# All 64 quads written out, lane 1's sort placed behind lane 0's quads, and gathers of 128 successive edges

## The chip, the cores and the metric

The kernel runs on one core of one Trainium2 chip. The metric is the device time of one launch in microseconds. Most runs of one kernel agree within 0.3%; the three runs of the kernel before lie between 25,302.51 and 25,315.38 us, with a median of 25,311.82.

The engines are named as in the profile: PE is TensorE (PEld its weight loads), DVE is VectorE, ACT is ScalarE, POOL is GpSimd, SP is SyncE. Each takes its instructions in order, and they wait for each other through semaphores. SP and ACT issue plain DMAs; POOL issues the indirect ones, in which each of 128 partitions fetches its own row.

## The reference

A graph layer over V = 100,000 nodes with 64 channels and E = 3,300,000 edges (1.6 million random pairs in both directions, and a loop at each node), sorted by target:

```python
h = jnp.maximum(_layernorm(x, axis=-1), 0.0)
local, nbr = h[dst], h[src]
y = jnp.concatenate([local, nbr - local], axis=-1) @ W.T + b      # per edge
s = segment_sum(y, dst); cnt = segment_sum(ones, dst)
out = x + where(cnt > 0, s / maximum(cnt, 1), 0)
```

Since the layer is linear, it is enough to have, for each target, the sum of h[src] over its edges and the count; the two halves of W are applied once per node. On average a node has 33 edges, and their sources are random. So the work is a gather of 3.3 million rows and a sum over sorted targets.

## The kernel before

**Start.** h is computed and written to DRAM as `h3`, each value as three bf16 parts (192 columns, and a column of ones for the count: CE = 193). `bounds` reads the targets of all chunks (below) and finds each chunk's lowest target (`base_r`, `base_b`) and whether a chunk spans more than 128 nodes; if any assumption fails, a flag in `odd` sends the kernel through a general slow loop behind everything else (`n_slow`).

The edges are then summed in two ways.

**Windows, in quads.** The first 2,039,808 edges are cut into 256 windows of 7,968 successive edges (some 241 nodes each). Four windows make a quad, so there are 64 quads. The two *lanes* hold 128 windows each, one per partition. Three functions work on them:

- `sort_lane(l, ...)` (L432 on) loads a lane's targets and sources, packs both in one 32-bit key, and sorts the 8,192 keys of each partition by *source*, in a network of exchanges: ACT copies the lower half of a piece to `tmp` (L470), DVE writes the minimum and the maximum back (L471, L472). A piece has up to PIECE = 1536 elements, and `tmp` is in PSUM. Positions of block limits are counted by ACT (L548) and DVE (L603). The sorted keys go to DRAM (`ksort`).
- `fill_lane(l, ...)` (L636 on) fetches from `ksort`, for each of 157 blocks of 640 nodes, the keys of each window whose source is in the block (161 indirect DMAs at L651 and 64 at L736), and writes what the quads need to DRAM: source places `sr_d`, target places `dt_d`, and the rest `et_d`, `xs_d`.
- `quads(base, n, kept)` (L754 on) goes over 157 blocks and one last step per quad, two steps at a time ("a pair of steps"; 79 pairs a quad). SP loads a piece of the table of all rows (`tab`, 727.5 KB for three blocks; two loads more for `srs` and `dt`). DVE makes two one-hots, `gh` (L806) and `dh` (L348). TensorE picks rows by `gh` (L828, six matmuls of 128 x 128 per block), ACT casts the result to `gs` (L830), and TensorE adds it to the targets by `dh` (L836, sixteen matmuls of 32 rows per block). The last step adds the edges of a node to itself and the spilled keys, and takes the four sums out of PSUM, into tiles `wsums` (8 buffers) that SP writes to `acc`. With `kept`, one table piece in five stays in SBUF.

**Chunks, by gathers.** The other 1,260,192 edges are cut into 352 chunks of 3,584 edges. `chunks(first, n, dynamic)` (L353 on) gives each partition 28 successive edges. Gather j (L403, an indirect DMA on POOL) takes edge j of each partition: 128 rows of `h3`. A one-hot `hot` of 128 x 128 for each gather (L348; DVE makes 14 at a time, a half chunk, in 4 buffers) gives the target relative to the chunk's lowest, and a matmul adds the rows to 128 sums (L408). `nb`, the gathered rows of a half chunk, has 6 buffers, so POOL runs up to six halves ahead of TensorE. There are 352 x 28 = 9,856 gathers.

**Order.** `sort_lane`, `fill_lane`, `quads` and `chunks` are generators: each `yield` hands back to the code that interleaves them, and a planner then puts the instructions in an order on each engine, close to that of the program, but with those ahead that are ready early; `issue_after(last[...])` (`behind()`) pins some to their places. The order is:

1. Lane 0's sort with gathers (`gathers(ns)`: one gather per GATHER = 1250 ns of the yields' own estimates), then lane 1's sort with lane 0's fill and gathers. Each lane has its own `keys` buffer.
2. Quads 0 to 3 with lane 1's fill and gathers; then the rest of the first PA = 70 chunks.
3. A loop `For_i` of three rounds: each holds 20 quads written out, and 94 chunks spread over them. Quad and chunk numbers are registers there.

The last lines of step 3 in the code:

```python
with tc.For_i(0, (SETS - U0) // SB, 1) as g:
    last.clear()
    ev = chunks(None, KB, PA + g * KB)
    next(ev)
    owed = 0.0
    for _ in quads(U0 + g * SB, SB, kept):
        owed += 2 * (KB * J - 1) / (SB * NE)
        while owed > 0:
            next(ev, None)
            owed -= 1
    drain(ev)
    add_now(True)
```

**End.** Rows shared by neighbouring windows or chunks are added, the means are taken and multiplied by the second half of W, and the result is written (L1065 to L1085).

## Time and profile before

| | us |
|---|---|
| median of three runs | 25,311.82 |
| lowest and highest run | 25,302.51, 25,315.38 |
| the profiled execution: its run | 25,318.98 |
| the profiled execution: span, first to last instruction | 25,317.3 |

The profile is of one execution. Busy time is the union of an engine's instructions; a matmul's end is modelled. "Idle before" is an engine's time without work just before a group, with what ended it: "<-issue" means that no semaphore was waited for, "<-remote" that the profile doesn't know who. The granted TensorE clock has a mean of 0.723. Three groups that the change touches, from the page's list of the costliest (line, engine, operation, output<-input, shapes, count | busy us, mean ns | idle us before, who ended it):

```profile
L403 POOL DMA_INDIRECT nb<-h,si x9856 | 9337.3, 947 | 13259.9 <-PE ps L408 8539.2
...
L348 DVE TENSOR_TENSOR hot<-near,c 128x1792 bf16<-128x1792 int16 x704 | 759.5, 1079 | 113.6 <-remote 107.4
...
L651 POOL DMA_INDIRECT kf<-ksort,at_i x322 | 306.6, 952 | 205.8 <-ACT k L692 108.3
```

### The profile page before, as it was taken

How to read it: one execution, taken by the hardware profiler on the slowest of the kernel's cores; microseconds unless marked ns; L12 is line 12 of the kernel's file. 1: busy time of each engine (PE TensorE's matmuls, PEld its weight loads, DVE VectorE, ACT ScalarE, POOL GpSimd, SP SyncE). 2: the span in 40 equal slices, each digit the busy share in tenths (PEclk: the TensorE clock that was granted, in tenths of full speed). 3: DMA queues.
4: the chain of work that ended last, by engine and by line, in shares of the span. 5: the costliest groups of instructions: out<-in, count | busy, mean ns of one | idle time of the engine just before them, and what ended most of it. 6: DMA issues, size and time to landing. Idle time of an engine off the chain costs nothing. (4 is left out here: it accounts for less than half of the span.)

```text
span 25317.3 us, 562905 instructions
## 1 busy us (share of the span) xinstructions
PE 14841.3 (59%) x238778; PEld 10732.9 (42%) x238778; DVE 11321.0 (45%) x15478; ACT 6060.7 (24%) x11710; POOL 10302.7 (41%) x10609
## 2 busy tenths in 40 slices
PE   4100365466666666665666666666566666666666
PEld 3000244344444444444444444444444444444445
DVE  6878443243444444443444444444344444444444
ACT  4333221122222222221222222222222222222222
POOL 5666533433333333334333333333333333333334
PEclk6555577677777777777777777777777777777777
DMA  6722354354454454454444544444445444444446
GB/s 227 102 46 46 100 172 147 108 151 143 145 149 145 147 149 143 149 153 134 147 143 147 149 146 148 149 147 145 138 144 148 145 150 146 150 145 145 148 145 231
DMA packets 1671411, 3615.08 MB, mean 143 GB/s; under 512 B 951932, under 2 KB 960263, under 8 KB 1663911
## 3 DMA queue, kind: packets, MB, share of 16 engines
q1 hardware_dynamic: 1225338, 3006.63, 36.6%
q0 software_dynamic: 335040, 507.40, 10.5%
q10 hardware_dynamic: 108492, 64.90, 1.3%
q8 instruction: 1874, 30.70, 0.5%
q14 instruction: 667, 5.46, 0.1%
HBM read 3397.56 MB, written 219.36 MB: 143 GB/s over the span
## 5 line engine op out<-in xcount | busy, mean ns | idle before, releaser
L403 POOL DMA_INDIRECT nb<-h,si x9856 | 9337.3, 947 | 13259.9 <-PE ps L408 8539.2
L348 DVE TENSOR_TENSOR dh<-dt,c 128x1024 bf16<-128x1024 int16 x5056 | 3450.9, 683 | 12561.4 <-remote 7908.4
L830 ACT CAST gs<-gp 128x386 bf16<-128x386 f32 x10048 | 4786.8, 482 | 16980.7 <-remote 9615.5
L836 PE MATMUL total<-gs,dh 32*128 32x193 bf16 x160768 | 6254.9, 264 | 4279.4 <-issue 4266.3
L828 PE MATMUL gp<-tab,gh 128*128 128x193 bf16 x48408 | 6076.5, 270 | 2426.6 <-issue 2187.6
L828 PEld LDWEIGHTS <-gh 128*128 128x128 bf16 x60288 | 5384.1, 105 | 4772.8 <-issue 4394.3
L836 PEld LDWEIGHTS <-dh 32*128 32x128 bf16 x160768 | 3875.8, 99 | 6281.3 <-issue 6228.6
L806 DVE TENSOR_TENSOR gh<-srs,c 128x1536 bf16<-128x1536 int16 x5056 | 4760.5, 942 | 15.0 <-issue 7.9
L408 PE MATMUL ps<-nb,hot 128*128 128x193 bf16 x9856 | 1934.7, 281 | 2839.1 <-DVE sums L422 1230.1
L408 PEld LDWEIGHTS <-hot 128*128 128x128 bf16 x9856 | 1048.8, 111 | 3031.1 <-DVE sums L422 1261.7
L828 PE MATMUL gp<-kept,gh 128*128 128x193 bf16 x11880 | 1551.9, 274 | 505.0 <-issue 493.1
L470 ACT COPY tmp<-keys 128x1536 f32<-128x1536 f32 (+14 forms) x540 | 649.6, 1212 | 1324.0 <-DVE keys L472 602.4
L348 DVE TENSOR_TENSOR hot<-near,c 128x1792 bf16<-128x1792 int16 x704 | 759.5, 1079 | 113.6 <-remote 107.4
L471 DVE TENSOR_TENSOR keys<-tmp,keys 128x1536 f32<-128x1536 f32 (+14 forms) x540 | 756.6, 1420 | 88.8 <-ACT junk L548 41.4
L472 DVE TENSOR_TENSOR keys<-tmp,keys 128x1536 f32<-128x1536 f32 (+14 forms) x540 | 756.3, 1419 | 22.4 <-issue 7.1
L795 POOL DMA_INDIRECT rows_x<-h,xs x128 | 120.8, 944 | 985.0 <-DMA xs<-xs_d 930.5
L651 POOL DMA_INDIRECT kf<-ksort,at_i x322 | 306.6, 952 | 205.8 <-ACT k L692 108.3
L856 DVE SCALAR_TENSOR_TENSOR whole<-own,whole 128x193 f32<-128x193 bf16 x512 | 190.3, 413 | 88.3 <-ACT whole L852 87.8
L420 DVE TENSOR_REDUCE sums<-ps 128x64 f32<-128x192 f32 x349 | 122.1, 350 | 209.5 <-remote 197.0
L310 PE MATMUL o_ps<-w_own,hT 128*128 128x128 f32 x784 | 186.7, 376 | 14.4 <-ACT hT L305 13.8
L310 PEld LDWEIGHTS o_ps<-w_own,hT 128*128 128x128 f32 x784 | 154.8, 251 | 77.8 <-ACT hT L305 68.2
L736 POOL DMA_INDIRECT kx<-ksort,xat x128 | 120.7, 943 | 88.5 <-DVE xat L733 43.5
(184 smaller groups left out, 3297.5 us busy)
## 6 DMA issues: line engine op xcount, KB each, us to landing
tab<-tables SPq DMA_DIRECT2D x2668, 727.5 KB
srs<-sr_d SPq DMA_DIRECT2D x1216, 512.0 KB
nb<-h,si POOLq DMA_INDIRECT x9856
tables<-h ACTq DMA_DIRECT2D x157, 242.5 KB
h<-parts SPq DMA_DIRECT2D x28, 1358.0 KB
acc<-zeros SPq DMA_DIRECT2D x28, 910.0 KB
at<-acc SPq DMA_DIRECT2D x28, 910.0 KB
xt<-in_x SPq DMA_DIRECT2D x28, 896.0 KB
```

The lines of the kernel that those rows point to most:

```text
L310: nc.tensor.matmul(o2[:, i], lhsT=hT[:, i], rhs=w_own.rearrange("p a c -> p (a c)"), start=False, stop=True)
L348: nc.vector.tensor_tensor(out.rearrange("p k (a d) -> p k a d", d=D), numbers[:, :, None].to_broadcast(shape), upto[:shape[0], :n].rearran ...
L403: last[POOL] = nc.gpsimd.indirect_dma_start(out=nb[:, j], out_offset=None, in_=h3, in_offset=bass.IndirectOffsetOnAxis(ap=si[:, u, at:at + ...
L408: nc.tensor.matmul(ps, lhsT=before[0][:, j], rhs=before[1][:, j, :CE], start=before[2] == 0 and j == 0, stop=before[2] == parts - 1 and j ...
L470: last[ACT] = nc.scalar.copy(tmp, lo)
L471: nc.vector.tensor_tensor(lo, tmp, hi, ALU.min)
L472: last[DVE] = nc.vector.tensor_tensor(hi, tmp, hi, ALU.max)
L651: last[POOL] = nc.gpsimd.indirect_dma_start(out=kf[:, c], out_offset=None, in_=ksort, in_offset=bass.IndirectOffsetOnAxis(ap=at_i[:, c0 + ...
L806: nc.vector.tensor_tensor(gh[:, :m].rearrange("p c i b s -> p (c i) b s"), srs[u, s // SL][:, c:c + m].rearrange("p c i s -> p (c i) s")[: ...
L828: nc.tensor.matmul(gp[:, i], lhsT=ghots[t][:, i, b], rhs=row[:, b + i * (NB - NR), :CE], start=b == 0, stop=b == NR - 1)
L830: nc.scalar.copy(gs[t], gp)
L836: nc.tensor.matmul(total[:, i, to(b)], lhsT=hot[at, b * P:b * P + P], rhs=of[at], start=flags.get("start", False) and b == 0, stop=flags.g ...
```

## The change

- **Gathers.** A gather takes 128 successive edges of a chunk in place of one edge from each of 128 runs (the host lays `src_p` and `dst_p` out anew). Its targets then lie near 4j above the chunk's lowest, so the one-hot is only BAND = 32 columns wide, relative to that drift. It is written into a strip of zeros (four tiles `narrow`, kept for the whole kernel), and the matmul reads a window of 128 columns of the strip, placed so that the band falls on the right targets. `bounds` checks the band in place of the span. The buffers of `nb` go from 6 to 5.
- **Order.** Only lane 0 is sorted ahead of the quads. Quads 0 to 31 follow, written out: lane 0's fill runs beside quad 0, ahead of it by two pieces, and lane 1's sort and fill run behind the rest (`behind_quads`), paced by their estimates. In lane 1's sort (`soft`) the pieces are of 1,024, `tmp` is a single buffer in SBUF, the copy on ACT and the minimum and maximum on DVE are two pairs of steps apart, no order is pinned, and ACT makes all the counts. There is one `keys` buffer for both lanes.
- Then quads 32 to 63, written out, with the kept tables, and the remaining gathers spread evenly. There is no loop, so no number of a quad or a chunk is a register.
- `dh` gets 5 buffers and also holds the one-hots of the last step, four at a time (`eh` had its own tile); `wsums` goes from 8 buffers to 5; quad 0 loads what its last step needs later (`late`).

```diff
-SB = 20
-KB = 94
-U0 = 4
+PARTS = (32, 32)
+U1 = 32
-STEP = 1300
+STEP = 2200
+BEHIND = 1.0
+BAND = 32
-EXTRA = 350
-PIECE = 1536
+PIECE = (1536, 1024)
-PART = 1024
+PART = 512
...
+            e = pre.tile([P, CHUNK], I32, name="e", bufs=1)
+            nc.vector.tensor_tensor(e[:n].rearrange("c (p j) -> c p j", j=J), d[:n].rearrange("c (p j) -> c p j", j=J),
+                                    drift_i[:n, None, :].to_broadcast([n, P, J]), ALU.subtract)
+            nc.vector.tensor_reduce(off[:n, 1, m:m + 1], e[:n], axis=AX.X, op=ALU.min)
...
+                nc.vector.tensor_sub(rel[:, :k], rel[:, :k], drift[:, None, :].to_broadcast([P, k, J]))
...
+            narrow = [[few.tile([P, JH * (P + D) + JH * D], BF16, name=f"hot{part}{i}") for i in range(2)]
+                      for part in range(J // JH)]
+            for hot in narrow[0] + narrow[1]:
+                nc.vector.memset(hot, 0.0)
...
-                    hot = rows.tile([P, JH, P], BF16, name="hot", bufs=4)
+                    hot = narrow[part][q % 2]
                     nb = rows.tile([P, JH, CT], BF16, name="nb")
                     with behind():
-                        one_hot(hot, near[:, u, part * JH:part * JH + JH], P)
+                        one_hot(hot[:, part * JH * D:][:, :JH * (P + D)].rearrange("p (k x) -> p k x", x=P + D)[:, :, :BAND],
+                                near[:, u, part * JH:part * JH + JH], BAND)
...
-                        nc.tensor.matmul(ps, lhsT=before[0][:, j], rhs=before[1][:, j, :CE],
+                        nc.tensor.matmul(ps, lhsT=before[0][:, BAND // 2 + j * P:BAND // 2 + j * P + P], rhs=before[1][:, j, :CE],
...
             def exchange(lo, hi, tmp):
-                last[ACT] = nc.scalar.copy(tmp, lo)
-                nc.vector.tensor_tensor(lo, tmp, hi, ALU.min)
-                last[DVE] = nc.vector.tensor_tensor(hi, tmp, hi, ALU.max)
+                ins = nc.scalar.copy(tmp, lo)
+                if not soft:
+                    last[ACT] = ins
+
+                def finish():
+                    nc.vector.tensor_tensor(lo, tmp, hi, ALU.min)
+                    ends_at(nc.vector.tensor_tensor(hi, tmp, hi, ALU.max))
+
+                return finish
+
+            def both(part, n):
+                finish = part()
+                if soft:
+                    yield 0
+                    yield 0
+                finish()
+                yield 2.083 * n + 290
...
+                    dh = hots.tile([P, 2, 2, CH], BF16, name="dh", bufs=5)
...
+                    begin = fill_lane(0, fill, took)
+                    for _ in range(4 * SL):
+                        next(begin)
+                    rest = behind_quads()
+                    left = 0.0
+                    for i, _ in enumerate(quads(0, U1, late=True)):
+                        if i < NE // 2 - 10:
+                            for _ in range(4):
+                                next(begin, None)
+                            gathers(STEP / 2)
+                        else:
+                            drain(begin)
+                            left += BEHIND
+                            while left > 0:
+                                left -= 1 + next(rest, 0) / 1500
+                            gathers(STEP)
                     drain(rest)
...
+                pace = (NCH * J - count[0]) / ((SETS - U1) * NE // 2 - 4)
+                owed = 0.0
+                for _ in quads(U1, SETS - U1, kept):
+                    gathers(pace * GATHER)
+                drain(ev)
+                add_now(True)
...
+    def by_gather(a):
+        return np.ascontiguousarray(a.reshape(nch, J, P).transpose(0, 2, 1))
```

`took()` counts each fetch of keys as a gather, so gathers pause while a lane is filled.

## The prediction

> **What bounds the kernel now.** I read the page's busy times first, then a table of windows by stage, then the timeline inside the loop, because no engine on the page is full.
>
> ```profile
> PE 14841.3 (59%) x238778; PEld 10732.9 (42%) x238778; DVE 11321.0 (45%) x15478; ACT 6060.7 (24%) x11710; POOL 10302.7 (41%) x10609
> ...
> q8 instruction: 1874, 30.70, 0.5%
> ```
>
> Busy shares give no bound here. The table by stage (start and end, length, then busy time and count of PE, PEld, DVE, ACT, POOL, granted clock, DMA share, GB/s) shows where the time is: lane 0's sort, lane 1's sort, the four quads ahead of the loop, leftover gathers, the loop, the tail.
>
> ```profile
> 430.00:1601.00 1171.00, 119.74 (x739) 103.71 (x740) 1047.49 (x989) 427.33 (x466) 768.36 (x787) 0.53 0.51 84
> 1601.00:2768.00 1167.00, 95.96 (x554) 73.45 (x552) 862.35 (x1146) 397.43 (x448) 757.79 (x798) 0.52 0.25 46
> 2768.00:4290.00 1522.00, 901.77 (x14225) 629.88 (x14223) 654.56 (x1127) 344.37 (x673) 609.86 (x644) 0.71 0.56 164
> 4290.00:4640.00 350.00, 70.66 (x655) 53.89 (x656) 41.23 (x72) 7.90 (x17) 219.44 (x234) 0.56 0.23 49
> 4640.00:24942.00 20302.00, 13185.85 (x219861) 9464.68 (x219861) 8305.74 (x11673) 4578.33 (x9654) 7531.60 (x7981) 0.75 0.49 146
> 24942.00:25318.00 376.00, 199.29 (x1184) 180.02 (x1181) 145.31 (x261) 57.06 (x115) 211.34 (x64) 0.76 0.73 277
> ```
>
> Sixty of the 64 quads fill 20,302 us, 338 us each. Two neighbouring windows in the loop, and POOL's timeline there, say why:
>
> ```profile
> 15074.00:15090.00 16.00, 15.69 (x314) 13.09 (x315) 11.93 (x17) 6.64 (x14) 0.94 (x1) 0.86 0.67 195
> 15090.00:15108.00 18.00, 6.68 (x53) 2.74 (x50) 1.71 (x3) 0.96 (x2) 12.26 (x13) 0.65 0.47 135
> ```
>
> ```profile
> 15088.79 0.94 POOL L403 DMA_INDIRECT nb<-h,si  x1 [17.14 <-PE ps L408]
> 15090.04 0.94 POOL L403 DMA_INDIRECT nb<-h,si  x1 [0.31 <-issue]
> ```
>
> With POOL quiet, TensorE starts 314 matmuls in 16 us; while POOL issues gathers, 53 in 18 us, and it waits for no semaphore ("issue"). The gathers come in bursts of 14, one every 1.25 us, when TensorE has freed a half chunk's rows (the wait for PE ps). I counted matmul starts from the records between 4800 and 11,200 us: inside bursts (shifted by 2.5 us, since data moves after the issue) 2.2 per us, outside 19.05. So gathers and quads nearly exclude each other, and the time is a sum of two prices. A quad has 3,666 matmuls (2,592 of L836, 942 of L828, 132 of L408): 3,666/19.05 = **192.4 us a quad**. A gather takes 1.25 x (1 - 2.2/19.05) = **1.10 us of TensorE** if it falls beside quads, and none beside a sort. Check: 60 x 192.4 + 7,981 x 1.10 = 20,323 against 20,302, loop starts included. The four early quads: 770 + 644 x 1.10 = 1,478 against 1,522. The loop alone would fit 1.08, so I use 1.09.
>
> **The change, part by part,** against the profiled span of 25,317.3 us (its run took 25,318.98, the median of three is 25,311.8, so 6 us come off at the end).
>
> *Lane 1's sort leaves the front.* Quads start at 2768 now. They can start when lane 0's sort is done and the first piece is filled. Lane 0's first fetch from the sorted keys is issued at 1601.6, but 146 us of lane 1's DVE work was done before it (29 of its exchanges at 2 x 1.43 us, 46 us of its load, 17 us of its reductions). With one keys buffer that work comes later; DVE is 89% busy in the stage, so I take 110 of the 146. Eight fetches, their DVE work and two DMAs: some 35 us more. Start at about 1,525: **-1,243**. Bounds: -1,100 (nothing of the 146) to -1,290.
>
> *More gathers fall beside quads.* The number of gathers stays 9,856. The sort's yields add up to 870,100 ns, one gather per 1,250 ns: 696 are issued behind lane 0, and I take 710 with those that run ahead. So 9,146 fall beside quads, with both lanes' 450 fetches of keys (225 a lane, 322 + 128 in all) and the 128 of rows_x: 9,724 against 644 + 7,981 = 8,625. 1,099 x 1.09 = **+1,198**. Bounds: the price from 1.07 to 1.25, +1,176 to +1,374. Their forms (128 rows of 194 bf16 from random sources) don't change: successive edges share a target, not a source.
>
> *The leftover gathers (4290 to 4640) go*: 350 us in which TensorE had almost no quad work; the 234 gathers are in the count above. The new seam after quad 31, where pools are opened again, I set at 50 by the loop starts: **-300** (-350 to -250).
>
> *The loop goes.* The windows with its second and third start hold 5,161 and 5,030 matmuls, their neighbours 5,450 and 5,440; at 10.9 per us that is 27 and 38 us: **-65** (-65 to 0). Written-out code costs no fetches: 1,874 packets of 16 KB carry 64 B for each of TensorE's 477,556 instructions, so the loop's code was fetched anew every time round already.
>
> *The one-hot of 32 columns.* Now 128 x 1792 elements in 1,079 ns, 704 times. A quarter of it is 448 elements, and the dh of 512 elements takes 421 ns, so about 0.4 us: 0.68 us saved a time, 480 us of DVE. But DVE waits for TensorE at nearly every dh (0.4 to 0.5 us), so most is hidden; in 5,000 us of the loop TensorE waits about 130 us for DVE in all. I take **-60** (-250 to 0). The weights stay 128 columns wide, so TensorE's price is unchanged. The extra subtraction in load is 44 x 0.4 us, hidden by DVE's slack.
>
> *Lane 1's sort and fill run behind quads 0 to 31.* 327,679 element pairs in 339 pieces of up to 1,024: 678 min/max at about 1.15 us (1,024 elements take 1.215) = 780 us; load 60; the fill's DVE rows add up to 210: **1,050 us on DVE**, and 339 copies of about 1 us plus 146 us of counts on ACT. The pacing spends 2,016 of 2,459 pairs of steps on it. DVE needs 1.46 us a pair (gh and dh start 0.86 and 0.60 apart), TensorE 192.4/79 = 2.44, so 0.94 x 2,459 = 2,300 us of slack covers it. What is not covered: DVE runs in order, so a 2.3 us min/max delays the next gh, behind which TensorE's L828 waits; its lead is one to two pairs, and more with dh's five buffers. ACT's copy likewise stands ahead of a gs cast. Bounds 0 (all in the lead) to +1,050 (all exposed); the nearest row is 2768 to 3200, where a fill with 210 us of DVE ran beside 2,500 matmuls (131 us at 19.05) and 227 indirect DMAs (247 us). That makes 378 of 432 us; of the 54 left a part is the quads' start, so at most a quarter of the fill showed. I take a fifth: **+200**.
>
> *Lane 1's tmp is in SBUF, lane 0's in PSUM.* Beside a DVE operation with two SBUF inputs a gather is longer:
>
> ```profile
> 485.88 0.94 POOL L403 DMA_INDIRECT nb<-h,si  x1 [0.30 <-issue]
> 486.64 1.23 DVE L458 TENSOR_TENSOR own<-s,keys 128x1024 int32<-128x1024 int32 x1 [4.93 <-DMA s<-in_src_w]
> 487.13 1.56 POOL L403 DMA_INDIRECT nb<-h,si  x1 [0.31 <-issue]
> ```
>
> 0.62 us more. Bursts fill half of the first 32 quads, but DVE mostly waits in them: 678 x 0.25 x 0.62 = **+105** (0 to +420).
>
> The Trainium skill ("SBUF — State Buffer", Who interferes with whom) speaks against this move: a DVE instruction with two SBUF inputs contends with a GpSimd one that reads SBUF, and the later is blocked for the whole of the other. The 1.56 agrees in kind, not in size; by its full 1.15 us a time the term would be +195 instead.
>
> *Quad 0* fetches its keys while it runs, and its last step needs xs and et, which come behind 31 us of DVE (64 x 0.48) and 64 fetches of 1.25 us: **+60** (0 to +150). *The bounds* read each chunk once more, 3 passes of DVE beside loads: **+10** (0 to 30).
>
> Sum: -1,243 + 1,198 - 300 - 65 - 60 + 200 + 105 + 60 + 10 = -95: 25,222 in the profile's terms, **25,215** as a median, 0.4% faster.
>
> **The rivals.** *The sort is not hidden* (slower). Place: DVE's queue in quads 1 to 26. For it: DVE's 1.46 plus the sort's 0.43 to 0.52 a pair is close to the 2.07 us in which a pair runs when TensorE is warm. Against it: the row of 2768 to 3200. Half exposed: 25,215 + 525 - 200 = 25,540; all, 26,065. It turns the sign from 297 us exposed.
> *The sort is free*: it fits into bursts in which DVE sits still and lengthens none: 25,215 - 305 = 24,910. For it: in 5,000 us of the loop DVE stands at dh for 1,816 us, 151 times. Against it: it waits at dh, with the sort's pieces queued behind.
> *Tables*: quads 4 to 31 lose the kept fifth, 28 x 11 x 727.5 KB = 224 MB, 560 us at the 400 GB/s of busy slices; half unhidden gives 25,495. Against it: from 3400 to 4280, without kept tables, 19.1 matmuls per us outside bursts as in the loop.
> *Not what it says*: the gathers stop disturbing TensorE because of their new order. Half the price would be 19,900; nothing in the trace speaks for it, as the sources stay random.
>
> **How the numbers follow.** My sum 0.50 (its own range 25,080 to 25,360), not hidden 0.27, free 0.16, tables 0.05, the gathers' price gone 0.02. 24,900 to 25,650 takes the first whole, most of the free case and the tables, and the cheaper part of the exposed one. About 0.2% (50 us) can be told from no change: faster below 25,261: 0.64 of the first, the free one, the last: 0.50; within: 0.13; slower: the rest, 0.37.
>
> **What would show it.** Lane 0's first fetch of keys near 1,490, the first L828 near 1,525. Outside bursts 19 matmuls per us in the second half; in the first half 18 if the sort costs 200, 15 or less if it is exposed, with PE's L828 waiting for DVE gh or keys. Gathers beside keys' min/max over 1.5 us. I am wrong if a gather's 1.10 us differs, or if POOL issues far more than 710 gathers ahead of the quads.

## The result

| | us |
|---|---|
| before: median of 4 runs (range) | 25,307.17 (25,299.20 to 25,315.38) |
| after: median of 4 runs (range) | 171,500.22 (171,485.17 to 171,528.44) |
| ratio, 95% interval | 6.7769 (6.7651 to 6.7886) |
| after: the profiled execution's span | 171,493.9 |

The forecast was 25,215 us. The changed kernel takes nearly seven times as long. Its page says at once where. The rows of the slices that matter, and the first two of its groups (count | busy us, mean ns | idle before, who ended it):

```profile
span 171493.9 us, 888195 instructions
...
PE   4666650000000000000000000000000000000000
...
POOL 4334444444444444444444444444444444444444
...
L1098 POOL DMA_INDIRECT acc<-sums,ti x25792 | 40201.6, 1559 | 56741.3 <-ACT sums L1097 44966.4
L1076 POOL DMA_INDIRECT nb<-h,si x25792 | 31111.8, 1206 | 17865.3 <-DMA si<-in_src_a 10495.2
```

TensorE has work in the first six slices of forty and next to none in the others. The two groups have 25,792 instructions each and are not on the page of before at all. 25,792 = 1,612 x 16: they are the 16 gathers and the 16 accumulating stores of each round of the general loop (L1066 to L1098), the second way of computing the sums, which runs only when a flag in `odd` says that the fast way can't be trusted. Windows by stage of the changed kernel (start:end, length, then busy time and count of PE, PEld, DVE, ACT, POOL, granted clock, DMA share, GB/s): lane 0's sort, the quads with lane 1's sort, two stretches of the other quads, the end of the quads, then two windows behind them:

```profile
430.00:1600.00 1170.00, 125.53 (x759) 106.53 (x757) 900.55 (x967) 395.09 (x446) 771.98 (x817) 0.53 0.47 88
1617.00:4900.00 3283.00, 1856.33 (x27926) 1313.24 (x27927) 2050.79 (x3040) 1084.02 (x1973) 1172.65 (x1191) 0.73 0.50 147
4900.00:13300.00 8400.00, 5485.61 (x90858) 3895.53 (x90855) 3308.10 (x4901) 1892.35 (x3992) 3094.08 (x3280) 0.75 0.55 170
13300.00:24850.00 11550.00, 7295.22 (x112388) 5048.52 (x112388) 4084.65 (x6144) 2315.12 (x4894) 4742.85 (x5028) 0.72 0.45 135
24850.00:25206.00 356.00, 238.82 (x4146) 173.91 (x4147) 145.16 (x227) 83.49 (x176) 118.85 (x126) 0.76 0.49 141
25206.00:171110.00 145904.00, 8105.16 (x25805) 2656.72 (x25796) 22331.20 (x37088) 4105.39 (x25784) 71296.66 (x51574) 0.50 0.17 27
171110.00:171494.00 384.00, 202.73 (x1184) 182.33 (x1183) 140.01 (x236) 58.08 (x124) 227.82 (x75) 0.75 0.72 271
```

The sixth window is 145,904 us long: 1,612 rounds of 90.5 us. What is left is 25,206 + 384 = 25,590 us, 273 more than the 25,317.3 of before. So there are two things to explain: a flag that should not be set, and a remainder 1.1% slower where 0.4% faster was foretold. In the timeline of one round the accumulating stores stand one behind the other, some 3.9 us apart; each waits for sums that DVE makes only when the store four places ahead has landed (four buffers):

```profile
100000.78 1.56 POOL L1098 DMA_INDIRECT acc<-sums,ti  x1 [2.40 <-ACT sums L1097]
100004.01 0.36 DVE L1096 TENSOR_REDUCE sums<-ps 128x64 f32<-128x192 f32 x1 [3.52 <-DMA acc<-sums,ti]
100004.40 0.16 ACT L1097 COPY sums<-ps 128x1 f32<-128x1 f32 x1 [3.72 <-DVE sums L1096]
100004.69 1.55 POOL L1098 DMA_INDIRECT acc<-sums,ti  x1 [2.36 <-ACT sums L1097]
```

**Which flag.** The change gives `bounds` a new question: does each gather of 128 edges stay in its band of 32 columns? For the low side it takes, over all places of a chunk, the smallest (target - 4 x number of the gather), and sets the flag where `least` - that - 1 reaches 16. I worked this out from the edges themselves. In 351 of the 352 chunks the value is at most 7 on the low side and 6 on the high side, less than half of the limit. The last chunk has 2,208 edges; its other 1,376 places are filled with target V = 100,000. Its least target is 99,932. The filled places of gather 27 give 100,000 - 4 x 27 = 99,892, and 99,932 - 99,892 - 1 = 39: the flag is set. The change masks the filled places for the high side (`d < V` times e, ahead of the max), but the min stands before the mask.

Each group of the runs below had the kernel before beside it on the same chip, and in two groups of five the kernel before took about 15,400 us, in the other three about 25,600, like the 25,307 above; ratios are formed within a group.

### The profile page after: what moved, and what is told of

Same layout as the page of the kernel before. It is cut to its first block, busy times and chain, and to the rows that moved or that the text cites. A ratio compares the mean times of both kernels' runs of the same rounds, so it can differ in the third digit from the quotient of the medians.

```text
span 171493.9 us, 888195 instructions
## 1 busy us (share of the span) xinstructions
PE 23572.7 (14%) x264570; PEld 13599.5 (8%) x264570; DVE 33268.4 (19%) x52824; ACT 10177.3 (6%) x37719; POOL 81637.6 (48%) x62195
## 3 DMA queue, kind: packets, MB, share of 16 engines
q0 software_dynamic: 4874432, 2649.99, 13.5%
q8 instruction: 1872, 30.67, 0.1%
## 5 line engine op out<-in xcount | busy, mean ns | idle before, releaser
L1098 POOL DMA_INDIRECT acc<-sums,ti x25792 | 40201.6, 1559 | 56741.3 <-ACT sums L1097 44966.4
L1076 POOL DMA_INDIRECT nb<-h,si x25792 | 31111.8, 1206 | 17865.3 <-DMA si<-in_src_a 10495.2
L1094 PE MATMUL ps<-nb,same 128*128 128x193 bf16 x25792 | 8106.7, 332 | 137830.8 <-DVE same L1080 66492.3
L1096 DVE TENSOR_REDUCE sums<-ps 128x64 f32<-128x192 f32 x25792 | 9161.2, 356 | 87234.3 <-DMA acc<-sums,ti 87234.2
L418 POOL DMA_INDIRECT nb<-h,si x9856 | 9348.3, 948 | 13436.6 <-PE ps L423 10453.5
L1094 PEld LDWEIGHTS <-same 128*128 128x128 bf16 x25792 | 2657.0, 109 | 143276.6 <-DVE same L1080 73066.9
L1097 ACT COPY sums<-ps 128x1 f32<-128x1 f32 x25792 | 4105.7, 159 | 141845.5 <-DVE sums L1096 141543.0
L869 PE MATMUL gp<-tab,gh 128*128 128x193 bf16 x53952 | 7092.2, 275 | 3596.1 <-issue 2867.3
L869 PEld LDWEIGHTS <-gh 128*128 128x128 bf16 x60288 | 5509.1, 106 | 6176.3 <-issue 5581.3
L1080 DVE TENSOR_TENSOR same<-dr,di 128x2048 bf16<-128x2048 int32 x1612 | 5742.3, 3562 | 0.0
L1083 DVE TENSOR_TENSOR prior<-same,before 128x2048 f32<-128x2048 bf16 x1612 | 3694.7, 2292 | 55.5
L1085 DVE TENSOR_REDUCE first<-prior 128x16 f32<-128x2048 f32 x1612 | 3669.3, 2276 | 0.0
L869 PE MATMUL gp<-kept,gh 128*128 128x193 bf16 x6336 | 878.2, 279 | 411.2 <-issue 361.2
```

What stands on the lines that cost most here:

```text
L418: last[POOL] = nc.gpsimd.indirect_dma_start(out=nb[:, j], out_offset=None, in_=h3, in_offset=bass.IndirectOffsetOnAxis(ap=si[:, u, at:at + ...
L869: nc.tensor.matmul(gp[:, i], lhsT=ghots[t][:, i, b], rhs=row[:, b + i * (NB - NR), :CE], start=b == 0, stop=b == NR - 1)
L1076: nc.gpsimd.indirect_dma_start(out=nb[:, j], out_offset=None, in_=h3, in_offset=bass.IndirectOffsetOnAxis(ap=si[:, j:j + 1], axis=0))
L1080: nc.vector.tensor_tensor(same, dr.rearrange("q p j -> q j p"), di[:, :, None].to_broadcast([P, JA, P]), ALU.is_equal)
L1083: nc.vector.tensor_mul(prior, same, before[:, None, :].to_broadcast([P, JA, P]))
L1094: nc.tensor.matmul(ps, lhsT=same[:, j], rhs=nb[:, j, :CE], start=True, stop=True)
```

## Experiments on the flag

**pads** (15,400 group): the changed kernel with one constant changed.

```
-        "dst_p": by_gather(padded(dst[n:], nch * CHUNK, V)),
+        "dst_p": by_gather(padded(dst[n:], nch * CHUNK, V + P)),
```

> The changed kernel, with the 1,376 empty places behind the last chunk's 2,208 edges filled with target V + P instead of V. Theory 1 (the padding trips the new band check): with V, the last chunk's least target is 99,932 and its smallest target less 4 x gather number is 100,000 - 108 = 99,892, so least - that - 1 = 39, over the limit of 16; with V + P it is at most 7, no flag is set, the general loop does no round, and the time is that of the changed kernel's quads plus its tail: 25,206 + 375 = 25,580 (25,400 to 25,750). Rival 2 (another flag, or a chunk whose edges really leave the band): the general loop still runs its 1,612 rounds, 171,500.

Measured: 16,433.99 us, ratio 1.0681 (1.0664 to 1.0698). The page of pads has no group of the general loop: the padding sets the flag, and nothing else does. The absolute number was foretold for a chip on which the kernel before takes 25,310, and is no test of it. **pads_2** repeated it in a 25,600 group.

> The padded version once more. Where the kernel before takes 15,400: 16,434 again. Where it takes 25,600: the twin with a third buffer for si and xs took 1.0142 of it, and the part of the changed kernel's own profile ahead of the general loop, 25,206 + 375, gives 1.011; theory: 1.010 to 1.016. Rival (the third buffers saved time there too): above 1.02.

Measured: 25,922.24 us beside 25,566.96, ratio 1.0143 (1.0125 to 1.0161), inside its range. This is the change with its flaw mended: 1.4% slower.

**forced** (15,400 group): the kernel before, with its flag set always.

```
-            nc.vector.tensor_scalar(odd[:, 0:1], odd[:, 0:1], float(P), None, op0=ALU.is_ge)
+            nc.vector.tensor_scalar(odd[:, 0:1], odd[:, 0:1], 1.0, None, op0=ALU.is_ge)
```

> The kernel before, with the limit of its span check lowered from 128 to 1 so that the flag is always set and the general loop computes the sums once more. Theory 1: the price of the general loop has nothing to do with the new order or gathers: 25,310 + 1,612 x 90.45 = 171,100 within 1%. Rival: the changed kernel's state makes the loop slow; then clearly less here.

Measured: 162,114.47 us, which is 146,714 over the 15,400.1 of before, 91.0 us a round beside 90.5. The general loop costs the same in the old order. My number for the sum was 5% too high, because it was made with the other base.

## Experiments on the remainder

**order_only** and **gathers_only** (15,400 group) take the change apart. order_only is the changed kernel with the old gathers, one-hots and check; gathers_only is the kernel before with the new ones, and V + P as fill.

```
 order_only
-                    hot = narrow[part][q % 2]
+                    hot = rows.tile([P, JH, P], BF16, name="hot", bufs=4)
...
-        "src_p": by_gather(padded(src[n:], nch * CHUNK, 0)),
+        "src_p": padded(src[n:], nch * CHUNK, 0).reshape(nch, P, J),
 gathers_only: the same places, the other way round, in the kernel before
```

> The changed kernel with the old gathers: edges spread over a chunk by column as before, one-hots of 128 columns, the old check of the span. No fill of the last chunk can trip that check. Theory 1: 25,630 (the padded version's 25,580 plus the 50 that the prediction gave to the narrow one-hot and its check). Rival 2 (the new order of the work, not the band check, sets a flag): 171,500. Rival 3 (the narrow one-hot costs time): below the padded version.

> The kernel before, in its old order with its loop, with the new gathers alone (128 successive edges, 32 columns, the band check, empty places at V + P). The prediction's terms give 25,310 - 60 + 10 = 25,260 (25,060 to 25,340): DVE saves 0.68 us 704 times, mostly hidden. Rival: DVE's queue paces the loop more than was thought, then up to -480: 24,830. If the gathers disturbed TensorE less in their new order, far less than 24,800.

Measured: order_only 16,477.73, ratio 1.0705 (1.0686 to 1.0724), so 44 us above pads; gathers_only 15,379.73 beside 15,400.1, ratio 0.9987 (0.9975 to 1.0000). Both put the narrow one-hot and its check at a gain of 20 to 44 us, beside the -60 + 10 of the prediction. In that group all of the loss, 1,034 us in pads, is the order's. Neither was run in a 25,600 group, so there it is not shown.

**half_old**, **half_new**, **half_old_2** leave out every second gather of the loop (half_old, 3,948 of them) or of the changed order behind the 28th chunk (half_new, 4,536), with the matmuls kept. These three were run once each, and so were forced, rows64 and nokept_old.

```
-                        last[POOL] = nc.gpsimd.indirect_dma_start(
+                        if dynamic is None or j % 2 == 0:
+                            last[POOL] = nc.gpsimd.indirect_dma_start(
...
-                        nc.tensor.matmul(ps, lhsT=before[0][:, j], rhs=before[1][:, j, :CE],
+                        nc.tensor.matmul(ps, lhsT=before[0][:, j], rhs=before[1][:, j if dynamic is None else j - j % 2, :CE],
```

> The kernel before; in its loop each second gather is left out, and the matmul of an edge row that was not fetched reads its neighbour's row instead (so the sums are others; the number of matmuls is the same). Some 3,950 gathers fewer. On a chip where the kernel before takes 15,400, theory: gathers take nothing from TensorE there (20 matmuls per us while they run), so 15,300 to 15,450. On one where it takes 25,310, theory: 1.09 each, 21,000; rival, 1.27 to 1.40 each as the quads of the changed kernel fit: 20,300 to 19,800. Rival for the first: GpSimd's 1.25 us each holds the loop there too, then some 5 per cent less.

> The padded version; from the 29th chunk on each second gather is left out and the matmul of an edge row that was not fetched reads its neighbour's row (other sums, same number of matmuls): 4,536 gathers fewer. Theory (GpSimd's issue holds quads 33 to 62): they fall from 215 to the 183 to 187 us of the old loop, quads 7 to 31 from 207 to about 198 as in the old order without kept tables, 1,100 us in all: 15,200 to 15,400. Rival (gathers are as free as they were in the old order, 147 us for 3,950; the order of DVE's work or the tables set the quads): 16,250 to 16,350.

> The kernel before with each second gather of its loop left out (3 x 94 x 14 = 3,948; the matmul of an edge row that was not fetched reads its neighbour's row). Where the kernel before takes 25,600: at the prediction's 1.09 us a gather 4,300 less, 21,300; at the 1.3 that leaving out 4,536 gathers of the new order showed, 5,130 less, 20,470. Where it takes 15,400: 15,262 again.

Measured: half_old (15,400 group) 15,261.90 beside 15,408.84: 147 us for 3,948 gathers, 0.04 us each. There a gather costs the quads nothing. half_old_2 (25,600 group) 20,422.97 beside 25,566.96: 5,144 us, **1.30 us a gather**, not 1.09. half_new fell in a 25,600 group, for which its text had no number: 20,060.23, which is 5,904 below si3 of the same group, again 1.30 each. So the prediction's price was a fifth too low for the gathers at the margin, and its ranges for the price (1.07 to 1.25) did not reach it.

**rows64** (25,600 group): each gather behind the 28th chunk fetches 64 rows, not 128.

```
+                        m = P if q < 28 else P // 2
                         last[POOL] = nc.gpsimd.indirect_dma_start(
-                            out=nb[:, j], out_offset=None, in_=h3,
-                            in_offset=bass.IndirectOffsetOnAxis(ap=si[:, u, at:at + 1], axis=0))
+                            out=nb[:m, j], out_offset=None, in_=h3,
+                            in_offset=bass.IndirectOffsetOnAxis(ap=si[:m, u, at:at + 1], axis=0))
```

> The padded version; from the 29th chunk on each gather fetches 64 rows and not 128, and its matmul uses those 64 alone, so that half of these edges are left out of the sums; the number of gathers and of matmuls is the same. Where the kernel before takes 25,600: if the price of a gather goes by its rows (their descriptors or packets), 9,072 x 0.65 = 5,900 less than the padded version; if it goes by the instruction, within 300 us of it. Where it takes 15,400: 0 to 300 less than the padded version by either, as fewer packets share the DMA engines with the tables.

Measured: 26,431.24, which is 509 above pads_2 and not 5,900 below it. So halving the rows and the bytes does not lower the price. The packets are not halved: on the gathers' queue their number is the same in both runs, and only the time that they took is less (first pads_2, then rows64; packets, packet time in us, share):

```profile
q0 software_dynamic: 335040, 507.40, 10.2%
q0 software_dynamic: 335040, 282.12, 6.5%
```

Whether the price goes by the instruction or by its packets is therefore not told apart. That the time rose by 509 agrees with neither number; in the trace quads 7 to 62 are each some 9 us longer, and I have no cause for it.

**lanes3** (25,600 group) follows from that price: the kernel before with 96 quads and 1,904 gathers instead of 64 and 9,856.

```
-LANES = 2
-SB = 20
-KB = 94
+LANES = 3
+SB = 23
+KB = 2
...
-                add_later((LAG - 1) * J, put)
-                add_later((LAG - 1) * J + GAP, shared)
+                put()
+                shared()
```

> The kernel before with three lanes of windows and not two: 96 quads, 68 chunks and not 352 (1,904 gathers, 1,680 of them ahead of the loop), 4 rounds of 23 quads with 2 chunks each, and a quad's rows stored as soon as they are summed. Where the kernel before takes 25,600, theory (a gather beside quads 1.30 us, a quad alone 169): quads start 1,168 later, at 3,936; 96 x (169 + 7.5 for 5 to 6 DMAs) = 16,950; 390 for the last lane's fill beside the first quads, 132 for four starts of the loop, 376 behind: 21,780 (21,300 to 22,300). Rival (1.09 and 192.4, the prediction's split): 96 x 198.5 = 19,060, so 23,890. Where it takes 15,400 and a quad takes 183 us with its gathers for nothing: 22,600.

Measured: 22,112.59 us, ratio **0.8652** (0.8637 to 0.8666): faster than the kernel before and than even_3 (25,828) in that group, and inside its range of 21,300 to 22,300. Ten of its quads, with 20 indirect DMAs in all (window; columns as above):

```profile
6460.00:8250.00 1790.00, 1545.35 (x35286) 1274.86 (x35289) 1275.88 (x1751) 767.94 (x1608) 18.86 (x20) 0.93 0.73 238
```

A quad nearly alone takes 179 us, at 35,286 / 1,790 = 19.7 matmuls per us. With the 132 matmuls of its share of gathers (6.7 us at that rate) it would be 186. That corrects both splits: the prediction's 192.4 was 6 too high, and the 169 of lanes3's text is no quad alone but the foot of a line through quads with many gathers. The price per gather grows: from 186 to the 257 us that quads of half_old_2 take with 68 indirect DMAs it is 1.05 us each, and from there 1.30 for each one that the kernel before has more. The 1.05 is an estimate, a mean over the first 68 from traces of different groups: within half_old_2 the quads that are neither first nor last in a round have 58 to 79 indirect DMAs and lie on 1.14 to 1.31 us each, depending on where a quad is cut, so the low price belongs to the first ones. Why it grows is open. Where the kernel before takes 15,400, lanes3 was not run; at its text's 22,600 it would be far slower there.

**pinned** and **pace** (15,400 group) and **si3** and **even** (25,600 groups) ask what the order itself costs.

```
 pinned: the min and max of lane 1, and its copies likewise behind the gs cast
+        def at_quads(soft, of):
+            return tc.issue_after(last[of].ins) if soft and of in last else nullcontext()
...
+                    with at_quads(soft, "dh"):
                         nc.vector.tensor_tensor(lo, tmp, hi, ALU.min)
                         ends_at(nc.vector.tensor_tensor(hi, tmp, hi, ALU.max))
 pace
-STEP = 2200
+STEP = 2400
 si3 (and xs likewise)
-                si = index.tile([P, KG, J], I32, name="si")
+                si = index.tile([P, KG, J], I32, name="si", bufs=3)
 even: si3, STEP 2350, yield 1500 behind each fetch of keys, and
+                            if i == NE // 2 - 10:
+                                owed = 0.0
...
-                                left -= 1 + next(rest, 0) / 1500
+                                with tc.issue_after(last["dh"].ins):
+                                    left -= 1 + next(rest, 0) / 1500
```

> The padded version (fill V + P) with each piece of lane 1's sort tied behind the quad's own work at which it is written: its copy behind that pair's gs cast on ACT, its min and max behind that pair's dh on DVE. The order then has the 339 pieces in quads 1 to 21 and not all in quads 1 to 5. Theory (DVE is full in quads 1 to 6 because the sort was drawn together there): quads 1 to 6 fall from some 310 us and more to some 220, no later quad grows by over 20 us, the whole is 450 to 600 us below the padded version where that takes 16,434 (15,830 to 15,980), and 200 to 400 below it on a chip where the kernel before takes 25,310. Rival (the sort costs its DVE time wherever it stands): within 100 us of the padded version.

Measured: 16,157.48, ratio 1.0490 (1.0468 to 1.0512), 277 below pads, so half of what was expected. Quads 1 to 6 did fall, from 305 to 419 us each to 177 to 247. But quads 20 to 22 rose to 272, 450 and 293, where the fill of lane 1 had been drawn together with 305 indirect DMAs in one quad. The sort's place matters; "no later quad grows by over 20 us" was wrong.

> The padded version with STEP 2400 instead of 2200: some 9 per cent more gathers beside quads 0 to 31, fewer behind. Theory (quads 33 to 61, with 166 indirect DMAs at 1.25 us each = 207 of their 215 us, are held by GpSimd's issue): they fall to some 157 DMAs and 203 to 206 us, quads 7 to 30 keep their 206, the whole is 250 to 350 us lower: 16,080 to 16,190 where the padded version takes 16,434. Rival (something else sets the second half): within 60 us of it. On a chip where gathers take TensorE's time in any case: no change, since their number is the same.

Measured: 16,324.50, ratio 1.0592 (1.0571 to 1.0613), 110 below pads. Quads 33 to 61 fell as foretold, from 215.2 us and 165.6 indirect DMAs to 204.3 and 152.7; quads 12 to 30 rose from 206.7 to 215.5, which I had not expected, and took back half of the 314 us gained there; quads 1 to 11 took another fifth.

**nokept_old** (15,400 group): the kernel before without tables kept in SBUF.

```
-                for _ in quads(U0 + g * SB, SB, kept):
+                for _ in quads(U0 + g * SB, SB):
```

> The kernel before, with no tables kept in SBUF in its loop: all 53 groups of tables of a quad are loaded, not 42. Theory (table loads, which idle L828 most where all are loaded, hold the changed kernel's quads 7 to 31 at 206 us against 183): 60 x 23 us more, 16,780 where the kernel before takes 15,400; on a chip where it takes 25,310, at most 100 more, as most of each quad goes to gathers. Rival (what is longer in those quads is the sort's and fill's rest, or the order of DVE's work): within 150 us of the kernel before.

Measured: 16,186.18, 777 more for 60 quads, 13 us a quad. Theory and rival both miss: carried over from the old order to the new, which no run shows, tables would be some 13 of the 23 us by which quads 7 to 31 of the changed order are longer there. So in that group tables cost time. The prediction's rival "tables" was about the 25,300 case, and there nothing speaks for it: in the changed kernel the line through quads 12 to 30, which keep no tables, gives some 380 us at the 165.3 indirect DMAs of quads 33 to 61, which keep a fifth, and these take 379.7. In the second half of pads, where a fifth of the tables is kept, TensorE waits for tables all the same (waits of PE; us in total, times, longest):

```profile
PE gp L869 <- DMA tab<-tables: 959.6, 233, 30.9
```

and SP, which issues the table loads, suggests why (waits of SP in the same window, 9700 to 15400):

```profile
SPq L824 <- DMA rows_x<-h,xs: 549.4, 26, 32.9
SPq L369 <- DMA nb<-h,si: 367.2, 46, 30.2
```

SP stands at the loads of `xs` and `si` until gathers have read the old numbers; GpSimd is late (166 x 1.25 = 207 of a quad's 215 us), and the tables behind in SP's queue would be late with it. This is argued, not shown: SP's largest wait there is another, for free table buffers (1,039.6 us, none over 5.8), and si3, made to test it, fell in a 25,600 group.

> The padded version with a third buffer for si (numbers of the edges' sources) and for xs, and nothing else. Theory (in quads 33 to 62 TensorE waits 960 us for tables because SP, which issues them, stands 549 us at the load of xs and 367 us at that of si until gathers are done with the old numbers): these waits go, and with them 300 to 700 us: 15,730 to 16,130 where the padded version takes 16,434. Rival (GpSimd, with 166 x 1.25 = 207 us of issue a quad, sets these quads itself, and SP's waits only pass it on): within 100 us of it.

> The padded version with all that lane 1's sort and fill issue tied behind the dh of the step at which it is written, a fetch of keys counted as two steps, the debt of gathers forgiven once when lane 0's fill is out (STEP 2350), a third buffer for si and xs. Theory (on a chip with the kernel before at 15,400 three things cost the new order its gain: the sort drawn together in quads 1 to 5, GpSimd idle early and full late, and SP's queue held behind loads that wait for late gathers): 1527 of start + 400 for quad 0 + 31 x 212 + 32 x 197 + 430 behind = 15,230 (15,000 to 15,450), below the kernel before. Rival (table loads without kept hold quads 1 to 31 at 215 and more, and the rest gives only part): 15,500 to 15,900. On a chip with the kernel before at 25,310: gathers take TensorE's time however they are placed, so 200 to 400 below the padded version, no more.

> The version with an even pace once more, in the hope of a call in which the kernel before takes some 15,400. There, as foretold for the first run of it: 15,230 (15,000 to 15,450); rival, tables without kept hold quads 1 to 31: 15,500 to 15,900. Where the kernel before takes 25,600: 1.010 of it again.

> The version with an even pace a third time. Where the kernel before takes 15,400: 15,230 (15,000 to 15,450); rival, tables without kept hold quads 1 to 31: 15,500 to 15,900. Where it takes 25,600: 1.010 of it again.

Measured, all in 25,600 groups: si3 25,964.32, ratio 1.0142 (1.0126 to 1.0159), no different from pads_2's 1.0143; even 25,866.01, 25,827.83 and 25,828.03, ratios 1.0104 (1.0087 to 1.0121), 1.0106 (1.0088 to 1.0124) and 1.0104 (1.0087 to 1.0121). Evening out gains 0.4% of before's time there, 98 us beside si3 where 200 to 400 was said. The third buffers and the even pace were meant for the 15,400 case, and no group fell there again: that even beats the kernel before there is untested.

## Why the prediction was wrong

**The step that failed** is "The bounds read each chunk once more, 3 passes of DVE beside loads: +10". It priced the new check as an operation and never asked what it decides. What it decides, for the padded last chunk, is that the general loop runs: 145,904 us where +10 was put. pads, which changes only the padding, shows it. "Not what it says" was looked for only in the gathers' effect on TensorE. The general loop was described ahead of the prediction and got no row, no price and no chance among the rivals, though its place (`n_slow`) and the two numbers needed (a limit of 16, a drift of 4 x 27 = 108 over a chunk whose tail is all V) stand in the code. The price could have been bounded too: 25,792 gathers and as many stores, at no less than the 1.25 us per gather of before, are 64,000 us.

**The remainder**, where the kernel before takes 25,300 to 25,600, term by term, beside the 273 us that the changed kernel's own trace shows without the general loop (pads_2 against its own group: 355):

| term | foretold | measured | from |
|---|---|---|---|
| start of the quads | -1,243 | -1,150 | first L869 at 1,617.5, not 1,525 |
| gathers beside quads | +1,198 (1,099 x 1.09) | +1,301 (1,001 x 1.30) | 9,626 indirect DMAs counted from the first quad on, beside 8,625; the price of half_old_2 |
| leftover gathers, loop starts | -365 | not separated | the seam: quad 31 is 16 us over the line below, not 50 |
| narrow one-hot and bounds | -50 | -20 to -44 | gathers_only, order_only, in the 15,400 group |
| sort and fill behind quads, tmp | +305 | some +380 | quads 1 to 6 of the changed kernel against the line through quads 12 to 30 |
| quad 0 | +60 | +87 | the same line |

With the measured terms, and -365 as foretold, the sum is about +220: the sign turns by the start (+93), the price of gathers (+103) and the sort (+75), none of them large. The forecast for the remainder missed on three sizes, and in the sort's term also on the wait that sets the price, as shown below. The start is the term with the plainest miss: the first fetch of keys stands at 1,581.7 us, not 1,490. Fewer gathers were left beside quads than foretold because 784 and 29 fetches were issued ahead, not 710. Two of the prediction's figures were off without effect: its line through the loop's 60 quads gives 1.10 ((20,302 - 60 x 192.4) / 7,981), not 1.08, and 2.44 - 1.46 is 0.98, not 0.94.

**The price of a gather** came from an average: rate inside bursts against rate outside. For a change that adds gathers, the cost of one more counts. It shows where quads have different counts: in the changed kernel's trace quads 12 to 30 (86 to 142 indirect DMAs) lie on a slope of 1.25 to 1.28 us each, depending on where a quad is cut; the line of the table is 170.8 us + 1.267 each. In quads 33 to 61 nearly all counts are 156 or 170, too close for a slope. The trace of before had it too, roughly: counted by when they are issued, the 54 quads of the loop that are neither first nor last of a round hold 114 to 156, and lie on 1.22 to 1.47 us each, again by where a quad is cut. So the higher price could have been read ahead of the prediction, and its range should have been wider upward than 1.25.

**The sort's place** was taken from the pacing ("2,016 of 2,459 pairs of steps"). The order that came out has all 339 pieces between 1,963 and 3,720 us, in quads 0 to 5: nothing tied them to the quads' work. DVE in the changed kernel, 1950 to 3900 (operation count | busy us, mean ns | idle before):

```profile
L498 DVE TENSOR_TENSOR keys<-tmp,keys 128x1024 f32<-128x1024 f32 (+9 forms) x339 | 397.3, 1172 | 10.5
L497 DVE TENSOR_TENSOR keys<-tmp,keys 128x1024 f32<-128x1024 f32 (+9 forms) x339 | 395.5, 1167 | 32.1 <-ACT tmp L492 28.3 <-issue 3.1
L843 DVE TENSOR_TENSOR gh<-srs,c 128x1536 bf16<-128x1536 int16 (+1 forms) x393 | 370.8, 944 | 403.5 <-remote 317.2 <-PE gp L869 86.0
```

The whole sort, 792 us of DVE at 1.17 us a piece (foretold: 780 at 1.15), stands beside 393 of the 5,056 gh. What TensorE waits for in this window, and in a window as long behind them:

```profile
PE gp L869 <- ACT gs L871: 383.4, 241, 8.3
PE total L877 <- issue: 279.5, 355, 3.2
...
PE gp L869 <- DVE gh L843: 17.1, 9, 3.7
```

```profile
PE total L877 <- issue: 344.1, 467, 2.5
PE gp L869 <- issue: 285.6, 373, 2.7
```

In the first window the largest wait is for ACT's cast, in the second it is for nothing that the profile shows. Outside bursts 11.9 matmuls per us start in the first, 18.8 in the second: the sort is exposed by the prediction's own sign (15 or less). The prediction named both ("a 2.3 us min/max delays the next gh"; "ACT's copy likewise stands ahead of a gs cast"), gave the price to the first, and it is the second: the wait for the cast, 383 us, is as large as the whole excess of these quads. The cast is late because a copy to `tmp`, the one buffer of lane 1's sort, often stands ahead of it in ACT's program, and ACT waits there until DVE's max has read what the last copy left (ACT's largest wait, same window):

```profile
ACT tmp L492 <- DVE keys L498: 506.5, 259, 7.2
```

pinned, which puts these copies behind the cast and the min and max behind `dh`, takes both waits away: from 1950 to 3900 TensorE's wait for the cast is 674.0 us in pads and 1.5 in pinned, ACT's wait for the max 634.7 and none, and quads 1 to 6 are 739 us shorter (15,400 group). even, which puts the sort's steps behind `dh` but not its copies behind the cast, keeps 251 us of TensorE's wait for the cast from 2500 to 9200. A second buffer for `tmp` was not run. Spread out (even against si3), the sort still costs most of it: quads 2 to 20 take some 382 us with 150 indirect DMAs, quads 33 to 62 366 with 151, so 19 x 16 = 304 us.

**The Trainium skill's rule** on two SBUF inputs beside GpSimd ("SBUF — State Buffer", Who interferes with whom) is borne out in kind by gathers that grow beside lane 1's min and max, but hardly in the mean: from 1,963 to 3,720 us, where the whole sort runs, POOL's 497 instructions, all indirect DMAs, take 512 us, 1.03 each beside 0.95 for a gather over the whole of before; "gathers beside keys' min/max over 1.5 us" holds for single ones alone (POOL's timeline beside two of the sort's max and min):

```profile
2699.87 1.85 POOL L418 DMA_INDIRECT nb<-h,si  x1 [0.30 <-issue]
2702.03 0.94 POOL L418 DMA_INDIRECT nb<-h,si  x1 [0.30 <-issue]
2703.28 1.24 POOL L418 DMA_INDIRECT nb<-h,si  x1 [0.31 <-issue]
```

At 0.95 each the 497 would take 472 us, so some 40 us of POOL's time are more, where +105 was foretold. What that costs the quads was not measured apart.

**Right** were: that the number of gathers beside quads grows by some 1,000 and that this eats the shorter front; that the written-out code loads no more instruction packets (q8 moves 1,872 in pads beside 1,874; the loop's end was not measured by itself); some 19 matmuls per us outside bursts once the sort is over (18.7 from 5000 to 12800 us of the changed kernel, 18.3 behind); the small value of the narrow one-hot.

## What to carry to other kernels

A change that adds or rewrites a check has two prices: its instructions, and what it switches on. Work the check out by hand on the odd case (the padded tail, the last chunk) before pricing a single instruction, and give the fallback a row among the rivals. Where two engines share a price, take it from the slope over stretches with different counts, since an average hides what one more costs; and where the order is made by a planner, pacing counts are a wish until the trace shows the pieces where they were meant to be.

## What the hardware showed that I had not expected

The same program of before took about 15,400 us in two groups of runs and about 25,600 in three, each group agreeing within 0.5% but for one run of 32,137; the same number of chip stands beside a group of each kind, so it is not only the chip. The difference is TensorE while gathers run. In the slow case 53 matmuls start in 18 us beside 13 gathers, as shown ahead. Here is gathers_only, in the 15,400 group, over 16 us full of gathers:

```profile
8040.00:8056.00 16.00, 15.57 (x335) 12.85 (x336) 12.37 (x19) 7.26 (x16) 12.03 (x14) 1.00 0.91 316
```

335 matmuls beside 14 gathers, at full clock. The gathers themselves take 947 and 949 ns in the two cases, gh 942 in both, and a round of the general loop 90.5 and 91.0 us. So the gathers themselves, DVE's operations and the general loop are alike in the two cases, and TensorE beside indirect DMAs is not: the matmuls that start differ, and so does the granted clock (1.00 here, 0.65 in the 18 us shown ahead). Which of the two comes first is not shown. What sets a chip in the one case or the other stays open, and with it which of the versions is best: without gathers beside quads (lanes3) the kernel is 13.5% faster in the one, and in the other a gather beside quads costs the old order 0.04 us, while the new order is bound more by its tables and by GpSimd's 1.25 us an issue, as far as nokept_old and pace show.
